# Graph layer with residual layernorm: W's product first, inside the stage that forms A, and A's unscaled blocks as the stationary operand

## Chip, cores, metric

One core of one Trainium2 chip. The metric is the device time of one execution in microseconds, and the median over the runs of a kernel. "PE" is TensorE's matmul side, "PEld" its weight loads, "DVE" VectorE, "ACT" ScalarE, "POOL" GpSimd, "SP" the engine that issues loads; "ACTq" and "SPq" are the queues on which transfers are issued. A run is fast when it lies within 1.5% of the fastest run of its kernel.

## The reference, cut to what matters

```python
B, N, F_IN, F_OUT = (8, 4096, 256, 256)                  # all float32
HW = jnp.einsum('bnf,fo->bno', H, W)                      # H is x
A_norm = jax.nn.relu((A + A.T) * 0.5)                     # A is adj, 4096 x 4096
D = jnp.sum(A_norm, axis=1)
d_inv_sqrt = jnp.where(D > 0, D_safe ** (-0.5), 0.0)
L_norm = jnp.eye(N) - d_inv_sqrt[:, None] * A_norm * d_inv_sqrt[None, :]
out = jnp.einsum('nm,bmo->bno', L_norm, HW)
return _layernorm(x + jax.nn.relu(out), axis=-1)
```

## The kernel before

It has two stages. The first forms A = relu((adj + adj.T)/2) in blocks of 512 x 512 (PE transposes, VectorE adds, ACT applies ReLU and sums the rows), writes A to DRAM and loads the first half of x. The second takes the batches in two halves and computes (x.T L), then W. P is 128, S is 512, A is 4, NS is 8, NB is 32, FC is 2, HB is 4.

```python
def symmetrise(i, j, tij, tji):                          # first stage, one block
    sym = spool.tile([P, A, S], F32, tag="sym", ...)      # 3 buffers
    for a in range(A):
        pt = psum.tile([P, S], F32, tag="ps", ...)
        for c in range(A):
            nc.tensor.transpose(pt[:, c*P:(c+1)*P], tji[:, c, a*P:(a+1)*P], ident)
        nc.vector.tensor_add(sym[:, a, :], pt, tij[:, a, :])
        m = i * A + a
        nc.scalar.activation(sym[:, a, :], sym[:, a, :], AF.Relu, scale=0.5,
                             accum_out=deg_parts[:, m, j:j+1])
    nc.scalar.dma_start(a_norm[i][j], sym)                # runs of 8 KB
# ... degrees, d^-1/2 as columns and along the free axis ...
for h in range(HALVES):                                   # second stage
    for j in range(NS):
        # pz: 8 PSUM banks, one for each (b, c)
        for i in range(NS):
            lt = npool.tile([P, A, S], F32, tag="lap", ...)
            nc.sync.dma_start(lt, a_norm[i][j])
            for a in range(A):
                m = i * A + a
                nc.vector.scalar_tensor_tensor(           # A scaled on the fly
                    lt[:, a, :], lt[:, a, :], ndinv[:, m:m+1], drow[:, j, :], ALU.mult, ALU.mult)
                # ... the identity is added on the diagonal ...
                for b in range(HB):
                    for c in range(FC):
                        nc.tensor.matmul(pz[b, c], lhsT=xt[h, m][:, b, c*P:(c+1)*P],
                                         rhs=lt[:, a, :], start=(m == 0), stop=(m == NB - 1))
        # ... pz is copied to zt; then, for each 128 rows, W's product:
        #     matmul(po, lhsT=zt[b, c][:, a*P:(a+1)*P], rhs=w_sb[:, c, :]),
        #     max(.,0) + x, layernorm, write
```

## Time and profile before

| | before |
|---|---|
| median | 4148.6 us (4 runs, 4146.7 to 4150.4) |
| first stage, to the first product with A | 397 us |
| products with A (8192 instructions) | 3516 us |
| W's products between them | 221 us |
| last layernorm and write | 13 us |
| bytes moved | 337 MB |

The four rows in the middle follow one another on the chain of work that ended last, so they add up to the span. The prediction shows the lines from which they come.

### The profile page before, as it was taken

The numbers are of one execution on the slowest core, as the hardware profiler recorded it, in microseconds if no ns is written. First come the engines' busy times: TensorE is split into PE (matmuls) and PEld (weight loads), VectorE is DVE, ScalarE is ACT, GpSimd is POOL, SyncE is SP. The second block draws the span as 40 slices with busy tenths as digits, with TensorE's granted clock in tenths as the row PEclk, the third lists the DMA queues.
The fourth block names the chain that finished last, engine by engine and source line by source line (L and its number), as shares of the span: only waits on it lengthen the run. The fifth ranks groups of instructions, "written<-read, shape, count | busy, mean of one in ns | idle before, by whom it ended". The sixth has DMA issues, their size and how long they took to land.

```text
span 4147.6 us, 24473 instructions
## 1 busy us (share of the span) xinstructions
PE 3912.8 (94%) x10272; PEld 1919.8 (46%) x10272; DVE 849.9 (20%) x1863; ACT 212.3 (5%) x585; POOL 75.7 (2%) x71
## 2 busy tenths in 40 slices
PE   4445999999999999999999999999999999999998
PEld 4344444454545444454545444454545444454544
DVE  3344112021212112021203112030302112020202
ACT  4444000000000000000000000000000000000000
POOL 0000000000000000000000000000000000000000
PEclk7667999999999999999999999999999999999999
DMA  9998111111111111111233101111111101111110
GB/s 391 407 389 310 41 41 51 41 51 41 51 41 51 41 40 52 41 51 41 76 117 107 41 36 56 41 51 41 51 41 50 41 32 60 38 54 41 51 41 21
DMA packets 129406, 337.40 MB, mean 81 GB/s; under 512 B 6160, under 2 KB 71952, under 8 KB 104720
## 3 DMA queue, kind: packets, MB, share of 16 engines
q1 hardware_dynamic: 86016, 234.90, 15.7%
q10 hardware_dynamic: 43280, 100.93, 6.4%
q8 instruction: 81, 1.33, 0.1%
q14 instruction: 29, 0.24, 0.0%
HBM read 235.14 MB, written 100.66 MB: 81 GB/s over the span
## 4 chain that ended last, share of the span: by engine, by line
PE 91%; DMA 7%; DVE 1%; SPq 1%; POOL 0%; issue 0%; ACT 0%; POOLq 0%; DVEq 0%; ACTq 0%
PE z L202 85%; PE o L154 5%; DMA adj<-in_adj_dram 5%; PE tr L85 1%; DMA a_norm<-sym 1%; DMA x<-in_x_dram 1%; DVE sym L88 1%; SPq L64 1%; SPq L74 0%; POOL dinv L128 0%; PE drow_ps L137 0%; ACT sym L90 0%; DVE y L170 0%; DVE y L161 0%; DVE stats L165 0%
## 5 line engine op out<-in xcount | busy, mean ns | idle before, releaser
L202 PE MATMUL z<-lap,x 128*128 128x512 f32 x8192 | 3518.3, 592 | 0.0
L202 PEld LDWEIGHTS z<-lap,x 128*128 128x128 f32 x8192 | 1556.4, 190 | 1952.4 <-issue 1935.6
L194 DVE SCALAR_TENSOR_TENSOR lap<-lap,ndinv,drow 128x512 f32<-128x512 f32 x512 | 354.4, 746 | 2651.4 <-DMA lap<-a_norm 2649.4
L85 PE MATMUL tr<-ident,adj 128*128 128x128 f32 x1024 | 170.7, 346 | 211.5 <-DMA adj<-in_adj_dram 211.5
L85 PEld LDWEIGHTS tr<-ident,adj 128*128 128x128 f32 x1024 | 163.8, 186 | 218.1 <-issue 210.3
L219 ACT COPY zt<-z 128x512 f32<-128x512 f32 x64 | 37.5, 586 | 3684.4 <-PE z L202 3684.4
L154 PE MATMUL o<-w_sb,zt 128*128 128x256 f32 x1024 | 223.6, 379 | 0.0
L154 PEld LDWEIGHTS o<-w_sb,zt 128*128 128x128 f32 x1024 | 194.6, 190 | 33.3 <-issue 7.7
L88 DVE TENSOR_TENSOR sym<-tr,adj 128x512 f32<-128x512 f32 x256 | 163.5, 686 | 219.8 <-PE tr L85 141.1
L90 ACT ACTIVATE sym<-sym 128x512 f32<-128x512 f32 x256 | 158.9, 622 | 213.4 <-DVE sym L88 168.3
L168 POOL TENSOR_TENSOR rstd<-rstd,neg_half 128x4 f32<-128x4 f32 x64 | 69.5, 1087 | 3680.8 <-DVE rstd L167 3676.4
L221 DVE COPY zt<-z 128x512 f32<-128x512 f32 x64 | 44.3, 692 | 337.0 <-PE z L202 337.0
L170 DVE TENSOR_SCALAR y<-y,mv,rstd 128x256 f32<-128x256 f32 x256 | 88.4, 409 | 59.7 <-POOL rstd L168 59.7
L165 DVE BATCH_NORM_STATS2 stats<-y 128x6 f32<-128x256 f32 x256 | 97.8, 410 | 1.1
L161 DVE SCALAR_TENSOR_TENSOR y<-o,x 128x512 f32<-128x512 f32 x128 | 86.0, 672 | 17.0 <-PE o L154 16.5
L90 ACT ACTIVATION_READ_ACCUMULATOR sym<-sym 128x1 f32 x256 | 47.9, 187 | 0.0
L166 DVE BATCH_NORM_AGGREGATE mv<-stats 128x2 f32<-128x6 f32 x256 | 42.9, 171 | 0.0
L199 DVE TENSOR_TENSOR lap<-lap,ident 128x128 f32<-128x128 f32 x64 | 15.8, 286 | 0.1
L137 PE MATMUL drow_ps<-ident,dinv 128*128 128x128 f32 x32 | 5.3, 341 | 10.0 <-DVE dinv L129 10.0
L128 POOL TENSOR_TENSOR dinv<-safe,neg_half 128x32 f32<-128x32 f32 x1 | 5.4, 5442 | 385.1 <-DMA a_norm<-sym 385.1
L167 DVE TENSOR_SCALAR rstd<-mv 128x4 f32<-128x4 f32 x64 | 10.5, 164 | 0.1
L137 PEld LDWEIGHTS drow_ps<-ident,dinv 128*128 128x128 f32 x32 | 5.1, 181 | 10.2 <-issue 10.2
(15 smaller groups left out, 7.9 us busy)
## 6 DMA issues: line engine op xcount, KB each, us to landing
lap<-a_norm SPq DMA_DIRECT2D x128, 1024.0 KB, 4.8
adj<-in_adj_dram SPq DMA_DIRECT2D x64, 1024.0 KB, 13.9
a_norm<-sym ACTq DMA_DIRECT2D x64, 1024.0 KB, 7.4
x<-in_x_dram SPq DMA_DIRECT2D x64, 512.0 KB, 9.2
out_dram<-y ACTq DMA_DIRECT2D x64, 512.0 KB, 2.9
w_sb<-in_L_gnn_W_dram ACTq DMA_DIRECT2D x1, 256.0 KB, 5.5
```

The source lines that it names most:

```text
L85: nc.tensor.transpose(pt[:, c * P : (c + 1) * P], tji[:, c, a * P : (a + 1) * P], ident)
L88: nc.vector.tensor_add(sym[:, a, :], pt, tij[:, a, :])
L90: nc.scalar.activation(sym[:, a, :], sym[:, a, :], AF.Relu, scale=0.5, accum_out=deg_parts[:, m, j : j + 1],)
L154: nc.tensor.matmul(po[:, b - b0, :], lhsT=zt[b, c][:, a * P : (a + 1) * P], rhs=w_sb[:, c, :], start=(c == 0), stop=(c == FC - 1),)
L161: nc.vector.scalar_tensor_tensor(y[:, b0 : b0 + 2, :], po, 0.0, xt[h, m][:, b0 : b0 + 2, :], ALU.max, ALU.add)
L165: nc.vector.bn_stats(stats[:, b, :], y[:, b, :])
L166: nc.vector.bn_aggr(mv[:, b, :], stats[:, b, :])
L168: nc.gpsimd.tensor_tensor(rstd, rstd, neg_half[:, :HB], ALU.pow)
L170: nc.vector.tensor_scalar(y[:, b, :], y[:, b, :], mv[:, b, 0:1], rstd[:, b : b + 1], ALU.subtract, ALU.mult,)
L194: nc.vector.scalar_tensor_tensor(lt[:, a, :], lt[:, a, :], ndinv[:, m : m + 1], drow[:, j, :], ALU.mult, ALU.mult)
L202: nc.tensor.matmul(pz[b, c], lhsT=xt[h, m][:, b, c * P : (c + 1) * P], rhs=lt[:, a, :], start=(m == 0), stop=(m == NB - 1),)
L221: nc.vector.tensor_copy(zt[b, c], pz[b, c])
```

## The change

W is applied first: G = x W costs the same arithmetic as applying it last. G needs x transposed (PE) and is scaled by r = d^-1/2 of its rows when it leaves PSUM; it is stored in DRAM. These "projections", one for each 128 rows of x, run inside the first stage, a round of the outer loop after the row sums that they need. In the second stage a 128 x 128 block of A, unscaled, is the stationary operand, and 512 columns of G are the moving one. The other scalings are applied to the results, so VectorE no longer scales L. G has 8 x 256 = 2048 columns, HG is half of them (1024), and e holds the row sums. Two smaller parts of the change: the row sums are a VectorE reduction instead of a by-product of ReLU (tested by act_sums), and adj has five buffers instead of four (not tested by itself). The intent was to take W's product and the scaling out of the stage where PE is the bound, and into one where PE was half idle.

The diff, cut to its core:

```diff
@@ first stage
-                nc.scalar.activation(sym[:, a, :], sym[:, a, :], AF.Relu, scale=0.5,
-                                     accum_out=deg_parts[:, m, j : j + 1])
-            nc.scalar.dma_start(a_norm[i][j], sym)
+            nc.scalar.activation(sym, sym, AF.Relu, scale=0.5)
+            nc.vector.tensor_reduce(part[:, i * A : (i + 1) * A, j * A : (j + 1) * A],
+                                    sym.rearrange("p a (c q) -> p a c q", q=P), AX.X, ALU.add)
+            nc.scalar.dma_start(a_dram[i][j].rearrange("(a p) s -> p a s", p=P), sym)   # runs of 2 KB
+        def project(m):
+            xin = xpool.tile([P, B, F], F32, tag="xin", ...)                            # 2 buffers
+            nc.sync.dma_start(xin, x[:, m * P : (m + 1) * P, :].rearrange("b p f -> p b f"))
+            xt = xpool.tile([P, B, FC, P], F32, tag="xt", ...)
+            for b in range(0, B, 2):
+                pt = psum.tile(...)
+                ...  nc.tensor.transpose(pt[:, k, c, :], xin[:, b + k, c * P : (c + 1) * P], ident)
+                nc.scalar.copy(xt[:, b : b + 2], pt)
+            g = xpool.tile([P, G], F32, tag="g", ...)
+            for b in range(0, B, 2):
+                ...  nc.tensor.matmul(pg[...], lhsT=xt[:, b + k, c, :], rhs=w_sb[:, c, :], ...)
+                nc.scalar.mul(g[:, b * FO : (b + 2) * FO], pg, r[:, m : m + 1])
+            nc.scalar.dma_start(g_dram[m], g)
+        todo = []
         for i in range(NS):
             for j in range(i, NS):
                 ...
+                for _ in range(-(-len(todo) // (NS - j))):
+                    project(todo.pop(0))
+            degrees(i)
+            todo += range(i * A, (i + 1) * A)
+        for m in todo:
+            project(m)
@@ second stage
+    for m in range(NB):
+        load_g(0, m)                                      # 33 buffers of 4 KB a partition
+    for h in range(HALVES):
+        for i in range(NB):
+            lt = lpool.tile([P, NB, P], F32, tag="l", ...)  # 2 buffers, loaded in runs of 512 bytes
+            for m in range(NB):
+                for c in range(HG // S):
+                    nc.tensor.matmul(py[c], lhsT=lt[:, m, :], rhs=gt[h, m][:, c * S : (c + 1) * S], ...)
+            # y = G e - py; relu(r y); + x; layernorm; write
-        # (the kernel before: scaling of L, x.T L, copies, W's product)
```

More of the change, by code (lines that the diff above doesn't have):

```diff
@@ L39 @@
     FC = F // P
+    G = B * FO
     HALVES = 2
     HB = B // HALVES
+    HG = G // HALVES
     EPS = 1e-5
     const = ctx.enter_context(tc.tile_pool(name="const", bufs=1))
-    xpool = ctx.enter_context(tc.tile_pool(name="xpool", bufs=NB + 1))
     dram = ctx.enter_context(tc.tile_pool(name="dram", bufs=1, space=bass.MemoryType.DRAM))
@@ L52 @@
     nc.scalar.dma_start(w_sb, w.rearrange("(c p) o -> p c o", p=P))
-    deg_parts = const.tile([P, NB, NS], F32, name="deg_parts")
+    part = const.tile([P, NB, NB], F32, name="part")
     neg_half = const.tile([P, NB], F32, name="neg_half")
     nc.vector.memset(neg_half, -0.5)
-    a_norm = [
-        [dram.tile([P, A, S], F32, name=f"a_norm_{i}_{j}") for j in range(NS)] for i in range(NS)
-    ]
-    xt = {}
-    def load_x(h, m):
-        xt[h, m] = xpool.tile([P, HB, F], F32, tag="x", name=f"x_{h}_{m}")
-        nc.sync.dma_start(
-            xt[h, m],
-            x[h * HB : (h + 1) * HB, m * P : (m + 1) * P, :].rearrange("b p f -> p b f"),
-        )
-    with tc.tile_pool(name="adj", bufs=4) as apool, tc.tile_pool(name="sym", bufs=3) as spool:
+    e = const.tile([P, NB], F32, name="e")
+    r = const.tile([P, NB], F32, name="r")
+    a_dram = [[dram.tile([S, S], F32, name=f"a_{i}_{j}") for j in range(NS)] for i in range(NS)]
+    g_dram = [dram.tile([P, G], F32, name=f"g_{m}") for m in range(NB)]
+    with (
+        tc.tile_pool(name="adj", bufs=5) as apool,
+        tc.tile_pool(name="sym", bufs=3) as spool,
+        tc.tile_pool(name="xin", bufs=2) as xpool,
+        tc.tile_pool(name="stat1", bufs=2) as stat1,
+    ):
         def load_adj(i, j):
@@ L88, in symmetrise @@
                 nc.vector.tensor_add(sym[:, a, :], pt, tij[:, a, :])
-                m = i * A + a
-                nc.scalar.activation(
-                    sym[:, a, :],
-                    sym[:, a, :],
-                    AF.Relu,
-                    scale=0.5,
-                    accum_out=deg_parts[:, m, j : j + 1],
-                )
-            nc.scalar.dma_start(a_norm[i][j], sym)
-        m = 0
+            nc.scalar.activation(sym, sym, AF.Relu, scale=0.5)
+            nc.vector.tensor_reduce(
+                part[:, i * A : (i + 1) * A, j * A : (j + 1) * A],
+                sym.rearrange("p a (c q) -> p a c q", q=P),
+                AX.X,
+                ALU.add,
+            )
@@ new lines, in symmetrise, with degrees @@
+            nc.scalar.dma_start(a_dram[i][j].rearrange("(a p) s -> p a s", p=P), sym)
+        def degrees(i):
+            ms = slice(i * A, (i + 1) * A)
+            deg = stat1.tile([P, A], F32, tag="deg", name=f"deg_{i}")
+            none = stat1.tile([P, A], F32, tag="none", name=f"none_{i}")
+            nc.vector.tensor_reduce(deg, part[:, ms, :], AX.X, ALU.add)
+            nc.vector.tensor_scalar(none, deg, 0.0, None, ALU.is_le)
+            nc.vector.tensor_add(e[:, ms], deg, none)
+            nc.gpsimd.tensor_tensor(r[:, ms], e[:, ms], neg_half[:, :A], ALU.pow)
@@ new lines, in project @@
+        def project(m):
+            xin = xpool.tile([P, B, F], F32, tag="xin", name=f"xin_{m}")
+            nc.sync.dma_start(xin, x[:, m * P : (m + 1) * P, :].rearrange("b p f -> p b f"))
+            xt = xpool.tile([P, B, FC, P], F32, tag="xt", name=f"xt_{m}")
+            for b in range(0, B, 2):
+                pt = psum.tile([P, 2, FC, P], F32, tag="ps", name=f"xtr_{m}_{b}")
+                for k in range(2):
+                    for c in range(FC):
+                        nc.tensor.transpose(pt[:, k, c, :], xin[:, b + k, c * P : (c + 1) * P], ident)
+                nc.scalar.copy(xt[:, b : b + 2], pt)
+            g = xpool.tile([P, G], F32, tag="g", name=f"gt_{m}")
+            for b in range(0, B, 2):
+                pg = psum.tile([P, 2 * FO], F32, tag="ps", name=f"pg_{m}_{b}")
+                for k in range(2):
+                    for c in range(FC):
+                        nc.tensor.matmul(
+                            pg[:, k * FO : (k + 1) * FO],
+                            lhsT=xt[:, b + k, c, :],
+                            rhs=w_sb[:, c, :],
+                            start=(c == 0),
+                            stop=(c == FC - 1),
+                        )
+                nc.scalar.mul(g[:, b * FO : (b + 2) * FO], pg, r[:, m : m + 1])
+            nc.scalar.dma_start(g_dram[m], g)
@@ L100 @@
+        todo = []
         for i in range(NS):
+            pairs = NS - i
             for j in range(i, NS):
@@ L106 @@
                     symmetrise(j, i, tji, tij)
-                if m < NB:
-                    load_x(0, m)
-                    m += 1
-        while m < NB:
-            load_x(0, m)
-            m += 1
-    p2 = ctx.enter_context(tc.tile_pool(name="p2", bufs=1))
-    npool = ctx.enter_context(tc.tile_pool(name="npool", bufs=3))
-    ypool = ctx.enter_context(tc.tile_pool(name="ypool", bufs=3))
-    stat = ctx.enter_context(tc.tile_pool(name="stat", bufs=4))
-    deg = p2.tile([P, NB], F32, name="deg")
@@ L121 @@
-    nc.vector.tensor_reduce(deg, deg_parts, AX.X, ALU.add)
-    pos = p2.tile([P, NB], F32, name="pos")
-    nc.vector.tensor_scalar(pos, deg, 0.0, None, ALU.is_gt)
-    safe = p2.tile([P, NB], F32, name="safe")
-    nc.vector.tensor_scalar(safe, pos, -1.0, 1.0, ALU.mult, ALU.add)
-    nc.vector.tensor_add(safe, safe, deg)
-    dinv = p2.tile([P, NB], F32, name="dinv")
-    nc.gpsimd.tensor_tensor(dinv, safe, neg_half, ALU.pow)
-    nc.vector.tensor_mul(dinv, dinv, pos)
-    ndinv = p2.tile([P, NB], F32, name="ndinv")
@@ L131 @@
-    nc.vector.tensor_scalar(ndinv, dinv, -1.0, None, ALU.mult)
-    drow = p2.tile([P, NS, S], F32, name="drow")
-    for j in range(NS):
-        pd = psum.tile([P, S], F32, tag="ps", name=f"drow_ps_{j}")
-        for a in range(A):
-            m = j * A + a
-            nc.tensor.transpose(
-                pd[:, a * P : (a + 1) * P], dinv[:, m : m + 1].to_broadcast([P, P]), ident
-            )
-        nc.scalar.copy(drow[:, j, :], pd)
-    def finish(h, j, zt):
-        for a in range(A):
-            m = j * A + a
-            y = ypool.tile([P, HB, FO], F32, tag="y", name=f"y_{h}_{m}")
-            stats = stat.tile([P, HB, 6], F32, tag="stats", name=f"stats_{h}_{m}")
-            mv = stat.tile([P, HB, 2], F32, tag="mv", name=f"mv_{h}_{m}")
-            rstd = stat.tile([P, HB], F32, tag="rstd", name=f"rstd_{h}_{m}")
-            for b0 in range(0, HB, 2):
-                po = psum.tile([P, 2, FO], F32, tag="ps", name=f"o_{h}_{m}_{b0}")
-                for b in (b0, b0 + 1):
-                    for c in range(FC):
-                        nc.tensor.matmul(
-                            po[:, b - b0, :],
-                            lhsT=zt[b, c][:, a * P : (a + 1) * P],
-                            rhs=w_sb[:, c, :],
-                            start=(c == 0),
-                            stop=(c == FC - 1),
-                        )
-                nc.vector.scalar_tensor_tensor(
-                    y[:, b0 : b0 + 2, :], po, 0.0, xt[h, m][:, b0 : b0 + 2, :], ALU.max, ALU.add
-                )
@@ new lines @@
+                for _ in range(-(-len(todo) // (NS - j))):
[4 more added lines that the diff above has]
+            project(m)
+    gpool = ctx.enter_context(tc.tile_pool(name="gpool", bufs=NB + 1))
+    lpool = ctx.enter_context(tc.tile_pool(name="lpool", bufs=2))
+    ypool = ctx.enter_context(tc.tile_pool(name="ypool", bufs=2))
+    stat = ctx.enter_context(tc.tile_pool(name="stat", bufs=4))
+    gt = {}
@@ new lines, in load_g @@
+    def load_g(h, m):
+        gt[h, m] = gpool.tile([P, HG], F32, tag="g", name=f"g_{h}_{m}")
+        nc.sync.dma_start(gt[h, m], g_dram[m][:, h * HG : (h + 1) * HG])
+    for m in range(NB):
+        load_g(0, m)
+    for h in range(HALVES):
+        for i in range(NB):
+            lt = lpool.tile([P, NB, P], F32, tag="l", name=f"l_{h}_{i}")
+            for s in range(NS):
+                nc.sync.dma_start(
+                    lt[:, s * A : (s + 1) * A, :],
+                    a_dram[s][i // A].rearrange("(a p) s -> p a s", p=P)[
+                        :, :, (i % A) * P : (i % A + 1) * P
+                    ],
+                )
+            xr = ypool.tile([P, HB, F], F32, tag="xr", name=f"xr_{h}_{i}")
+            nc.sync.dma_start(
+                xr, x[h * HB : (h + 1) * HB, i * P : (i + 1) * P, :].rearrange("b p f -> p b f")
+            )
+            py = [psum.tile([P, S], F32, tag="ps", name=f"py_{h}_{i}_{c}") for c in range(HG // S)]
+            for m in range(NB):
+                for c in range(HG // S):
+                    nc.tensor.matmul(
+                        py[c],
+                        lhsT=lt[:, m, :],
+                        rhs=gt[h, m][:, c * S : (c + 1) * S],
+                        start=(m == 0),
+                        stop=(m == NB - 1),
+                    )
+                if i == NB - 1 and h + 1 < HALVES and m < NB - 1:
+                    load_g(h + 1, m)
+            y = ypool.tile([P, HB, FO], F32, tag="y", name=f"y_{h}_{i}")
+            yf = y.rearrange("p b o -> p (b o)")
+            for c in range(HG // S):
+                nc.vector.scalar_tensor_tensor(
+                    yf[:, c * S : (c + 1) * S],
+                    gt[h, i][:, c * S : (c + 1) * S],
+                    e[:, i : i + 1],
+                    py[c],
+                    ALU.mult,
+                    ALU.subtract,
+                )
+            nc.scalar.activation(yf, yf, AF.Relu, scale=r[:, i : i + 1])
+            nc.vector.tensor_add(y, y, xr)
+            stats = stat.tile([P, HB, 6], F32, tag="stats", name=f"stats_{h}_{i}")
+            mv = stat.tile([P, HB, 2], F32, tag="mv", name=f"mv_{h}_{i}")
+            rstd = stat.tile([P, HB], F32, tag="rstd", name=f"rstd_{h}_{i}")
@@ L178, in finish @@
             nc.scalar.dma_start(
-                out[h * HB : (h + 1) * HB, m * P : (m + 1) * P, :].rearrange("b p f -> p b f"), y
+                out[h * HB : (h + 1) * HB, i * P : (i + 1) * P, :].rearrange("b p f -> p b f"), y
             )
-    for h in range(HALVES):
-        for j in range(NS):
-            pz = {
-                (b, c): psum.tile([P, S], F32, tag="ps", name=f"z_{h}_{j}_{b}_{c}")
-                for b in range(HB)
-                for c in range(FC)
-            }
-            for i in range(NS):
-                lt = npool.tile([P, A, S], F32, tag="lap", name=f"lap_{h}_{j}_{i}")
-                nc.sync.dma_start(lt, a_norm[i][j])
-                for a in range(A):
-                    m = i * A + a
-                    nc.vector.scalar_tensor_tensor(
-                        lt[:, a, :], lt[:, a, :], ndinv[:, m : m + 1], drow[:, j, :], ALU.mult, ALU.mult
-                    )
-                    if i == j:
-                        diag = lt[:, a, a * P : (a + 1) * P]
-                        nc.vector.tensor_add(diag, diag, ident)
-                    for b in range(HB):
-                        for c in range(FC):
-                            nc.tensor.matmul(
-                                pz[b, c],
-                                lhsT=xt[h, m][:, b, c * P : (c + 1) * P],
-                                rhs=lt[:, a, :],
-                                start=(m == 0),
-                                stop=(m == NB - 1),
-                            )
-                if h + 1 < HALVES and j == NS - 1 and i < NS - 1:
-                    for a in range(A):
-                        load_x(h + 1, i * A + a)
-                if h > 0 and j == 0 and i == 1:
-                    for a in range(A):
-                        load_x(h, (NS - 1) * A + a)
-            zt = {}
-            for k, (b, c) in enumerate(pz):
-                zt[b, c] = ypool.tile([P, S], F32, tag=f"zt_{b}_{c}", name=f"zt_{h}_{j}_{b}_{c}", bufs=1)
-                if k % 2 == 0:
-                    nc.scalar.copy(zt[b, c], pz[b, c])
-                else:
-                    nc.vector.tensor_copy(zt[b, c], pz[b, c])
-            finish(h, j, zt)
+        if h + 1 < HALVES:
+            load_g(h + 1, NB - 1)
 _INS = ["x", "adj", "L0_gnn_W"]
```

## The prediction

> **What bounds the kernel now.** I read the slices of the span first, then the chain that ended last in order of time, then the groups, then short stretches of the timeline. The slices show two stages with different limits (each column is a fortieth of the span, 104 us):
>
> ```profile
> PE   4445999999999999999999999999999999999998
> PEclk7667999999999999999999999999999999999999
> DMA  9998111111111111111233101111111101111110
> GB/s 391 407 389 310 41 41 51 41 51 41 51 41 51 41 40 52 41 51 41 76 117 107 41 36 56 41 51 41 51 41 50 41 32 60 38 54 41 51 41 21
> ```
>
> In the first stage (not quite four slices) the DMA engines are full at about 390 to 407 GB/s and PE is under half busy, at a granted clock of 0.6 to 0.7. After that PE is full at full clock and the DMA nearly idle. The chain in order of time (start us, us, what) gives the second stage exactly:
>
> ```profile
> 397.45 219.74 PE z L202 x512
> 617.18 13.81 PE o L154 x64
> ...
> 3900.64 219.73 PE z L202 x512
> ```
>
> Sixteen rounds of 219.74 + 13.81 us = 3736.8 us lead without a gap from 397.45 to 4134.2; the last 13.4 us to 4147.6 are the last layernorm and its write. So the first stage costs 397, W's product (L154) costs 16 x 13.81 = 221 on the path, and the adjacency product costs 3516. The groups (busy us, mean ns of one, idle before):
>
> ```profile
> L202 PE MATMUL z<-lap,x 128*128 128x512 f32 x8192 | 3518.3, 592 | 0.0
> L85 PE MATMUL tr<-ident,adj 128*128 128x128 f32 x1024 | 170.7, 346 | 211.5 <-DMA adj<-in_adj_dram 211.5
> L154 PE MATMUL o<-w_sb,zt 128*128 128x256 f32 x1024 | 223.6, 379 | 0.0
> L88 DVE TENSOR_TENSOR sym<-tr,adj 128x512 f32<-128x512 f32 x256 | 163.5, 686 | 219.8 <-PE tr L85 141.1
> L90 ACT ACTIVATE sym<-sym 128x512 f32<-128x512 f32 x256 | 158.9, 622 | 213.4 <-DVE sym L88 168.3
> ```
>
> The source has 4096 matrix products at L202 and the profile has 8192 instructions, so an f32 product is two instructions; at 219.74/512 = 429 ns each for 512 columns, and 13.81/64 = 216 ns for 256 columns. The mean duration (592) overlaps its neighbours and isn't the rate. VectorE's scaling of L (354 us busy) and the copies hide behind PE, so dropping them alone buys nothing.
>
> **What the Trainium skill says.** (1) "TensorE: Matmul & The Clock Gate", Part 1: the array starts at half clock and gets the full one after some 3.4 us of sustained work. Two stretches of one burst of transposes agree (stretch, length, busy time and count of each engine, clock, DMA, GB/s): 0.55, then 1.00, at 190 and then 107 ns per transpose.
>
> ```profile
> 375.20:378.70 3.50, 3.42 (x18) 3.45 (x19) 1.97 (x3) 1.44 (x4) 0.00 (x0) 0.55 0.54 219
> 378.70:382.30 3.60, 3.52 (x33) 3.28 (x31) 3.60 (x7) 3.47 (x12) 0.00 (x0) 1.00 0.82 346
> ```
>
> Part 4 of that page says that transposes don't bring the full clock; this trace shows that they do. (2) "DMA: Bandwidth & Descriptors", Issuing engines are not separate DMA queues: transfers issued by SP and ACT share the same engines. The trace agrees: reads of adj and x on one queue and writes of A on the other together make the 390 to 407 GB/s; so added bytes are added time in this stage. (3) "ScalarE: Activation LUTs", What ACT_TABLE_LOAD costs: an ACTIVATE with immediates takes 186 ns + 0.833 ns per element, a scale from memory adds about 93. 186 + 427 = 613 against 622 measured: it agrees.
>
> **The change part by part.** *Adjacency product.* Per half 32 row blocks x 32 column blocks x 2 groups of 512 columns: 4096 products of 128x128 by 512 again. Which operand is stationary swaps, the count, width and data type stay: 8192 x 0.429 = 3516 us, unchanged. Its loads are 64 x 2 MB, about 38 GB/s over 55 us per row block, in runs of 512 bytes instead of 8 KB; even at a third of the first stage's rate 2 MB take 16 us of 55. They stay hidden with two buffers.
>
> *W's product* leaves the second stage: -221 us. It reappears in the first as 32 projections (one per 128 rows of x), each of 16 new transposes of x and 16 products (32 instructions): 16 x 0.107 + 32 x 0.216 = 8.6 us of PE at full clock. A block of A costs 16 x 0.107 = 1.7 us.
>
> *Bytes of the first stage.* Before: adj 67.1 + A 67.1 + half of x 16.8 = 151 MB in 385 us = 392 GB/s. After: all of x (33.6) and its product written (33.6): 201.3 MB, at the same rate 513 us, +128. A block (1 MiB in, 1 MiB out) and a projection (the same) cost 5.35 us of DMA each.
>
> *The first stage by rounds of its outer loop*, the larger of DMA and PE in each, because the projections lag by a round. Round 0: 15 blocks, no projection: 80.3 us. Rounds 1 to 5: 13, 11, 9, 7, 5 blocks and 4 projections each: (13+4) x 5.35 = 91, then 80.3, 69.6, 58.9, 48.2, all DMA (PE of the last is 43). Round 6: 3 blocks, 4 projections: DMA 37.5, PE 39.5. Round 7: 1 and 4: DMA 26.8, PE 36.1. The last 4 projections stand alone: PE 34.4. Sum 428.3 + 110.0 = 538.3, and 7 for the first load to land (the first transpose starts at 7.1 now) is 545. I add 25 for waits between engines and stretches of PE below full clock, a guess of under 5%: **570 us**.
>
> *Other engines in that stage.* VectorE: four adds of 0.64 us start to start (163.5/256) and a new reduction of 2048 elements per block. From a reduction of 256 elements that took 0.42 us and about 1.04 ns per further element (0.746 us for 512 in the scaling, less a fixed part), I estimate 2.3 us: 4.8 x 64 = 310 us. ACT: 64 x (186 + 0.833 x 2048 = 1.9 us) + 128 copies x 0.59 + 128 scaled copies x 0.7 + 96 issues x 0.33 = 320. Both are below 513, but in round 0 VectorE (72 us) is close to the DMA (80).
>
> *Handover.* Now the first load of the second stage goes out when the last write of A has landed:
>
> ```profile
> 385.14 0.33 ACTq L97 DMA_DIRECT2D a_norm<-sym  x1
> ...
> 389.09 1.29 SPq L191 DMA_DIRECT2D lap<-a_norm  x3
> ```
>
> So 4 us for the write, 4.8 median for the load. The scaled product's tiles take over the first stage's memory in the same way: about **10 us** from the last projection to the first product, as what was 12 us before (385 to 397). The 31 further tiles follow at 1.3 us each while PE uses 1.7 us per tile, so they don't hold it.
>
> *Between the halves* the new tiles are loaded behind the products that free the old; the blocks of A may queue behind them: **4 us**, the latency of one load. *The end*: two evictions at 0.69, ReLU 1.1, add 1.2, four pairs of statistics 2.3, power 1.0, four normalisations 1.4, latencies, and 4 us for the write: **13 us** as before.
>
> Sum: 570 + 10 + 3516 + 4 + 13 = 4113; I say **4115 us**, 0.8% less. Of the 221 us taken out of the second stage some 185 come back in the first, mostly as bytes.
>
> **Rivals.** *A: the first stage runs engine after engine.* If each engine followed the source strictly, VectorE would wait for the whole block's ReLU before its reduction (2.6 + 2.1 + 2.3 = 7 us per block), and ACT would sit in that ReLU while PE waits for its copies of x; a pair of blocks and a projection would take about 21 us where the DMA needs 16. Over the 28 projections that is 140 more, some 710 for the stage and 4250 in all. Against it: the order is not the source's. Between the halves now the source has four loads of x after each load of L, yet further loads of L were issued ahead of them:
>
> ```profile
> 1991.02 27.79 SPq L191 DMA_DIRECT2D lap<-a_norm  x2
> 2039.17 20.97 SPq L64 DMA_DIRECT2D x<-in_x_dram  x4
> 2060.23 0.46 SPq L191 DMA_DIRECT2D lap<-a_norm  x1
> ```
>
> So work that is ready goes first, and 3 to 5 buffers per kind should keep the DMA full most of the time. *B: PE is the bound, cold.* With transposes at 0.167 us (170.7/1024 now) and W's products at 0.3, a projection takes 12.2 us, rounds 3 to 7 become PE-bound, and the stage takes about 620: 4165. For it: the clock of 0.6 to 0.7 now; against: PE will have shorter pauses. *C: ACT is held by issuing its writes.* A's write now has runs of 2 KB, like adj's load, whose issue took up to 7.7 us with full queues, while the 8 KB write always took 0.33. At 3 us for each of 64, ACT has 490 us, near the bound: 4130 to 4180. *D: the handover hides nothing.* If all 32 tiles of the product (16.8 MB, 43 us) come before the first block of A, it costs 50 instead of 10: 4155. *E: it overlaps better*, with a stage of 535 and no gap at the handover: 4070.
>
> **Range and chances.** E gives the low end, B and D together or a mild A the high end: 4070 to 4210. The 2% lines are 4067 and 4233. Faster needs a first stage below 525, hardly more than the bytes alone take: 0.05. Slower needs one of 690, the strict serial order: 0.10. Same: 0.85.
>
> **What would show it.** The adjacency product should be 8192 instructions at 429 ns, without idle time of PE beyond a few us per half; if its rate is another, the largest term is wrong. W's group should have moved into the first 14% of the span, at 216 to 300 ns each. The DMA row should be 9 for over five slices at about 390 GB/s; if it sits well lower there with PE below 9 too, rival A or C holds, and the waits of VectorE and ACT, or long issues on ACT's queue, tell which. If PE stands at 9 in the slices before the second stage with a clock of 0.7, it is B. A gap of over 20 us before the first adjacency product is D.

## The result

4108.4 us median (4 runs, 4104.2 to 4111.8) against 4148.6 before: ratio 0.9903, 95% interval 0.9889 to 0.9918. A ratio, here and below, is the mean time of one kernel's fast runs over that of the other's of the same rounds, so it is not quite the ratio of the medians. The profiled run spans 4105.6 us.

The slices of the changed kernel (a column is 103 us):

```profile
PE   5788999999999999999999999999999999999998
PEclk6899999999999999999999999999999999999999
DMA  9999872221111211211121621112222211111220
GB/s 382 398 403 405 318 283 62 62 62 53 41 61 61 62 62 62 62 44 49 62 61 62 220 62 59 39 57 62 62 62 62 62 48 45 62 62 62 62 62 11
```

The first stage now takes five and a half slices. The DMA is full for the first four. In the next two the mean falls to 318 and 283 GB/s while PE's row rises to 9. How the bound passes from bytes to PE is plainer in four stretches (stretch, length, busy time and count of PE, PEld, DVE, ACT, POOL, clock, DMA share, GB/s):

```profile
400.00:450.00 50.00, 46.16 (x286) 40.89 (x283) 24.81 (x30) 28.75 (x38) 1.01 (x1) 1.00 1.03 390
450.00:500.00 50.00, 45.55 (x251) 39.91 (x250) 17.56 (x22) 28.15 (x40) 1.41 (x2) 0.94 0.82 286
500.00:535.00 35.00, 35.00 (x192) 31.33 (x192) 0.00 (x0) 18.84 (x32) 0.60 (x1) 0.98 0.68 234
535.00:567.00 32.00, 31.45 (x170) 27.83 (x168) 0.00 (x0) 16.70 (x28) 0.00 (x0) 1.00 0.49 175
```

The DMA stays full to about 450 us, beside a PE that is over 90% busy. From 500 us on PE is busy nearly all the time, VectorE has nothing more to do, and the DMA moves 234 and then 175 GB/s, about half of the 400 from before. The chain in order of time shows where the path changes hands, and the handover to the second stage:

```profile
388.75 22.31 DMA xin<-in_x_dram
...
549.14 1.75 PE xtr L116 x16
550.89 6.91 PE pg L123 x32
557.79 1.75 PE xtr L116 x16
559.54 6.92 PE pg L123 x32
567.21 3.79 DMA g<-gt
571.64 4.27 DMA g<-g
576.15 3517.78 PE py L179 x8192
```

The transfer that ends at 411 us is the last one on the path of the first stage until its last write; from there on the path is PE with short pieces of VectorE and ACT. A projection is 16 transposes (1.75 us) and 32 product instructions (6.91 us); at the end they stand back to back, and the last eight come after the transposes of the last block of A. Then the last piece of G is written (3.79 us), the first is loaded (4.27 us), and all 8192 instructions of the product with A follow without a gap, between the halves of the batches as well. They end at 576.15 + 3517.78 = 4093.9; 11.7 us of layernorm and write remain.

The groups that answer to those shown of before (busy us, mean ns, idle before):

```profile
L179 PE MATMUL py<-g,l 128*128 128x512 f32 x8192 | 3517.8, 592 | 9.7 <-DMA g<-g 9.7
L123 PE MATMUL pg<-w_sb,xt 128*128 128x256 f32 x1024 | 251.1, 403 | 41.7 <-ACT xt L117 39.2
L86 PE MATMUL tr<-ident,adj 128*128 128x128 f32 x1024 | 140.4, 300 | 65.4 <-DVE sym L89 34.7
L91 DVE TENSOR_REDUCE part<-sym 128x16 f32<-128x2048 f32 x64 | 143.7, 2277 | 9.2 <-ACT sym L90 9.1
L90 ACT ACTIVATE sym<-sym 128x2048 f32<-128x2048 f32 x64 | 122.5, 1914 | 166.8 <-DVE sym L89 165.4
```

| | before | after | difference |
|---|---|---|---|
| up to the first product with A | 397.4 | 576.2 | +178.7 |
| products with A, and W's between them | 3736.8 | 3517.8 | -219.0 |
| end | 13.4 | 11.7 | -1.7 |
| span of the profiled run | 4147.6 | 4105.6 | -42.0 |

So of 219 us taken out of the second stage 179 came back in the first. The question for the experiments is what holds the first stage.

### The profile page after: what moved, and what is told of

It is laid out like the page before. It is cut to its first block, busy times and chain, and to the rows that moved or that the text cites. A ratio compares the mean times of both kernels' runs of the same rounds, so it can differ in the third digit from the quotient of the medians.

```text
span 4105.6 us, 25348 instructions
## 1 busy us (share of the span) xinstructions
PE 3965.0 (97%) x10752; PEld 1947.4 (47%) x10752; DVE 687.9 (17%) x1369; ACT 346.3 (8%) x385; POOL 73.2 (2%) x78
## 4 chain that ended last, share of the span: by engine, by line
PE 91%; DMA 6%; DVE 2%; ACT 1%; issue 0%; SPq 0%; ACTq 0%; POOLq 0%; DVEq 0%
PE py L179 86%; PE pg L123 4%; DMA a<-sym 2%; DMA adj<-in_adj_dram 2%; DVE sym L89 1%; DMA xin<-in_x_dram 1%; PE tr L86 1%; DMA l<-a 1%; PE xtr L116 1%; ACT sym L90 1%; DVE part L91 0%; ACT xt L117 0%; DMA g<-g 0%; DMA g<-gt 0%; DVE stats L205 0%
## 5 line engine op out<-in xcount | busy, mean ns | idle before, releaser
L179 PE MATMUL py<-g,l 128*128 128x512 f32 x8192 | 3517.8, 592 | 9.7 <-DMA g<-g 9.7
L179 PEld LDWEIGHTS py<-g,l 128*128 128x128 f32 x8192 | 1557.1, 190 | 1970.0 <-issue 1968.8
L191 DVE SCALAR_TENSOR_TENSOR y<-g,e,py 128x512 f32<-128x512 f32 x128 | 95.7, 748 | 3058.3 <-PE py L179 3051.3
L199 ACT ACTIVATE y<-y,r 128x1024 f32<-128x1024 f32 x64 | 73.5, 1148 | 3455.2 <-DVE y L191 3455.2
L123 PE MATMUL pg<-w_sb,xt 128*128 128x256 f32 x1024 | 251.1, 403 | 41.7 <-ACT xt L117 39.2
L123 PEld LDWEIGHTS pg<-w_sb,xt 128*128 128x128 f32 x1024 | 201.3, 201 | 85.3 <-ACT xt L117 57.1
L91 DVE TENSOR_REDUCE part<-sym 128x16 f32<-128x2048 f32 x64 | 143.7, 2277 | 9.2 <-ACT sym L90 9.1
L90 ACT ACTIVATE sym<-sym 128x2048 f32<-128x2048 f32 x64 | 122.5, 1914 | 166.8 <-DVE sym L89 165.4
L130 ACT ACTIVATE gt<-pg,r 128x512 f32<-128x512 f32 x128 | 87.7, 690 | 103.4 <-PE pg L123 99.9
L200 DVE TENSOR_TENSOR y<-y,xr 128x1024 f32<-128x1024 f32 x64 | 78.5, 1226 | 77.8 <-ACT y L199 77.8
```

Of the source, the lines that this page charges most:

```text
L90: nc.scalar.activation(sym, sym, AF.Relu, scale=0.5)
L91: nc.vector.tensor_reduce(part[:, i * A : (i + 1) * A, j * A : (j + 1) * A], sym.rearrange("p a (c q) -> p a c q", q=P), AX.X, ALU.add,)
L123: nc.tensor.matmul(pg[:, k * FO : (k + 1) * FO], lhsT=xt[:, b + k, c, :], rhs=w_sb[:, c, :], start=(c == 0), stop=(c == FC - 1),)
L130: nc.scalar.mul(g[:, b * FO : (b + 2) * FO], pg, r[:, m : m + 1])
L179: nc.tensor.matmul(py[c], lhsT=lt[:, m, :], rhs=gt[h, m][:, c * S : (c + 1) * S], start=(m == 0), stop=(m == NB - 1),)
L191: nc.vector.scalar_tensor_tensor(yf[:, c * S : (c + 1) * S], gt[h, i][:, c * S : (c + 1) * S], e[:, i : i + 1], py[c], ALU.mult, ALU.subtract,
```

## Experiments

Twelve kernels ran, each three times timed beside the kernel before on the same chip, and once more with a profile. **Theory T**: the bytes hold the first stage up to some 430 us, then PE's projections do. **R1**: the bytes and the waits around them hold all of it. **R2**: VectorE and ACT waiting for each other hold it.

### no_pe: the projection without PE

```diff
-            (transposes, copies, products, scaled copies)
+            nc.scalar.mul(g[:, b * FO : (b + 2) * FO], xin[:, b : b + 2, :], r[:, m : m + 1])
```

> Wrong result on purpose: the projection keeps its load of x, its ACT work and its write, but has no transpose and no product on PE (G = r*x). Theory T (the first stage is held by the bytes for some 430 us and by PE's projections in its last 130 us): with PE out of the way the stage is bytes alone, 206.5 MB (with the 5 MB of the second stage's loads that go out early) at 397 GB/s = 520, and the first adjacency product starts at about 537 instead of 576: total 4067 +- 10. Rival R1 (the bytes and the waits around them hold the whole stage, PE's end part is only where the last bytes happen to be): no more than 10 us gained, 4095 or more. Rival R2 (VectorE and ACT waiting for each other hold it): also 4095 or more.

Measured: 4070.1 us, ratio to before 0.9812 (0.9797 to 0.9826). The first product starts at 540.65 (chain of no_pe):

```profile
536.08 4.57 DMA g<-g
540.65 3518.52 PE py L166 x8192
```

T holds: without PE's part the stage is 35 us shorter and not shorter than its bytes (206.5 MB at 397 GB/s are 520 us, the estimate of the expectation). R1 and R2 as sole causes are out, since all transfers and all of VectorE's work were still there (ACT's work fell by 70 us, from 346 to 277, as the copies went with the transposes). What is left, 541 us, is the bytes and some 20 us of waits that no run takes apart. So of the 179 us that came back, 143 (541 less 397) are there without PE's projections, and 36 are PE's.

### act_sums: row sums on ACT, no VectorE reduction

```diff
-            nc.scalar.activation(sym, sym, AF.Relu, scale=0.5)
-            nc.vector.tensor_reduce(part[...], sym..., AX.X, ALU.add)
+                nc.scalar.activation(sym[:, a, :], sym[:, a, :], AF.Relu, scale=0.5,
+                                     accum_out=part[:, i * A + a, j : j + 1])
```

> Right result: ReLU per 128x512 slice with the row sums taken by ACT, as in the kernel before, instead of one ReLU over the whole block and a VectorE reduction (144 us of VectorE taken out, some 85 us of ACT added). Theory T: VectorE isn't on the path that sets the end, and the bytes stay: within 8 us of 4108. Rival R2 (the wait of VectorE for the block's ReLU and its reduction hold the first 400 us): 20 us or more faster, 4088 or less.

Measured: 4108.1 us, ratio 0.9904 (0.9889 to 0.9919). Taking 141 us of busy time off VectorE (687.9 to 546.6; ACT got 43 more) changed nothing. R2 is out, and in this kernel the new row sums cost nothing.

### no_xt, no_xt3 and x3: a smaller projection, and its control

```diff
# no_xt: the transposes and their copies are left out; the products read x as it is
-                            lhsT=xt[:, b + k, c, :],
+                            lhsT=xin[:, b + k, c * P : (c + 1) * P],
# no_xt3: as no_xt, and; x3: only this
-        tc.tile_pool(name="xin", bufs=2) as xpool,
+        tc.tile_pool(name="xin", bufs=3) as xpool,
```

> Wrong result on purpose: only the 16 transposes of x per projection and the 4 copies behind them are left out, the W products stay. A projection takes 6.9 us of PE instead of 8.65. Theory T: the nine projections that stand alone at the end and some of those just before are each 1.75 us shorter, 16 to 24 us in all: 4082 to 4092. R1 and R2: within 5 us of 4108.

Measured: 4097.0 us (4093.5 to 4103.0), ratio 0.9880: 11 us gained, less than T's 16. Its chain shows PE waiting for x in the part where it should have been the bound:

```profile
485.13 10.29 DMA xin<-in_x_dram
...
502.74 7.86 DMA xin<-in_x_dram
...
524.81 6.89 DMA xin<-in_x_dram
```

The edit did more than it should: the products now read x itself, so its two buffers come free later. Hence no_xt3, in whose trace nothing waits for x any more.

> Wrong result on purpose: no transposes of x, as in no_xt, but with three buffers for x instead of two. In no_xt the load of x has to wait for the W products that now read it directly, and PE waited 25 us for x between 485 and 532 us. Theory T with that as the cause of the small gain: those waits go, and the gain against 4108 is 16 to 24 us: 4084 to 4092. Rival (the bytes bound the end part more than T has it): 4094 or more, as without the third buffer.

Measured: 4079.0 us, ratio 0.9835 (0.9820 to 0.9850): 29 us under the changed kernel, above the 16 to 24 expected. In the changed kernel fifteen projections, not nine to thirteen, stand between 413 and 566 us, and 15 x 1.75 = 26. But no_xt3 differs from the changed kernel in the buffer too, so its control was needed.

> Right result: the changed kernel with three buffers instead of two for x, its transposes and the product, and nothing else. It is the missing control of no_xt3 (4079), which has the third buffer and no transposes. Theory T: at the end PE itself is the bound, 8.65 us for each projection, so that a further buffer gives nothing: within 6 us of 4108, and the 29 us of no_xt3 are the transposes of some 15 projections (1.75 us each). Rival (the third buffer, that is earlier loads of x, gave a good part of those 29): 4098 or less.

Measured: 4139.2 us (4137.7 to 4144.4), ratio 0.9980: 31 us slower than the changed kernel, which neither theory had. In the traces the order of instructions (waits for semaphores left out) is the same on PE, VectorE and ACT and differs on SP alone. The waits of x3 (who waited for whom: us in total, times, longest) and then its chain:

```profile
PE py L179 <- DMA l<-a: 49.5, 1, 49.5
```

```profile
549.47 6.92 PE pg L123 x32
557.13 3.79 DMA g<-gt
...
596.07 9.41 DMA l<-a
605.83 3518.35 PE py L179 x8192
```

PE's first stage ends 10 us earlier than in the changed kernel, but then PE waits 49.5 us. The first block of A for the second stage is loaded behind all 32 tiles of G (16.8 MB). In the changed kernel that block was loaded between 40 and 120 us. The first stage's buffers there take 40 + 24 + 48 = 112 KB of a partition and G's 33 tiles 132 KB, so that the blocks of A lie in memory that the first stage doesn't use; with 136 KB they share it and must wait for its end. This is my reading from the buffer sizes and SP's order; the 49.5 us are measured. The other traces agree with it: in the seven kernels with at most 112 KB (the changed one, act_sums, no_pe, no_xt, no_xt3, early, early_half) the first block of A was loaded at 37 to 54 us, and in x3 and the three resident kernels below, where its memory is shared too, only at the end of the first stage (596, 776, 609 and 506 us). It is the prediction's rival D, put at 50 us instead of 10. In no_xt3 there is no xt, the buffers are 112 KB again, and the load is early. What the third buffer is worth by itself therefore stays open: x3's last seven projections stand back to back at 8.65 us each, so it doesn't speed those, and its 10 us earlier end also has 4.2 MB less to load (the 16 pieces of A), which is 10 us at 400 GB/s.

### early: projections spread from the first round on

```diff
-                nc.scalar.mul(g[:, b * FO : (b + 2) * FO], pg, r[:, m : m + 1])
+                nc.scalar.copy(g[:, b * FO : (b + 2) * FO], pg)
-                for _ in range(-(-len(todo) // (NS - j))):
+                done += 2 if j > i else 1
+                while todo and (NB - len(todo)) * NS * NS < done * NB:   # todo = all 32 from the start
                     project(todo.pop(0))
     def load_g(h, m):
         ...
+        nc.scalar.mul(gt[h, m], gt[h, m], r[:, m : m + 1])
```

> Right result: W's product is stored unscaled, so that projections need no row sums and are spread evenly from the first round on; the scale r is applied by ACT to each tile of the product when it is loaded in the second stage. No byte and no PE work is added or taken away. Theory T: PE's work now lies beside the bytes, and no projections stand alone at the end: the first adjacency product at 535 to 545 instead of 576, total 4065 to 4080. R1 and R2: the bytes or the order hold the stage anyway, within 8 us of 4108.

Measured: 4075.1 us (4072.9 to 4075.5), right result, ratio 0.9822 (0.9807 to 0.9836). One stretch of early (columns as above) and then its chain:

```profile
400.00:500.00 100.00, 84.25 (x502) 73.30 (x502) 60.66 (x71) 51.76 (x67) 3.02 (x3) 0.97 1.05 402
```

```profile
538.42 4.19 DMA g<-g
544.07 3517.97 PE py L181 x8192
```

The same work in another order, with 64 scalings by ACT added in the second stage, saves 33 us. The DMA is now full up to 500 us; in the last 30 us of the stage it still falls to 276 and 211 GB/s. That is 5 us from no_pe, where PE had nothing to do in the projections. T holds. A part of the gain is given back at the handover, where PE waits 13.3 us (9.7 in the changed kernel), as the first tile of G has to be scaled as well.

### early_half: 16.8 MB less to write

```diff
-            nc.scalar.dma_start(g_dram[m], g)
+            nc.scalar.dma_start(g_dram[m], g[:, :HG])
```

> Wrong result on purpose: the spread projections (label early), but only the first half of each row of W's product is written, and both halves of the batches read it. Nothing else differs: 16.8 MB of writes are gone from the first stage. Theory T (with the projections spread, the first stage is as long as its bytes): 16.8 MB at 400 GB/s = 42 us off, 4033 +- 10. Rival (once spread, PE and the order of the engines are as close a bound as the bytes; PE was 0.74 to 0.88 busy there): 4055 or more.

Measured: 4036.8 us (4033.3 to 4042.1), ratio 0.9734 (0.9719 to 0.9748): 38 us less than early for 16.8 MB, where 42 were expected from the rate. The first product starts at 502.29. So once the projections are spread, bytes are time, at nine tenths of the rate.

### resident, resident2 and resident3: half of G never leaves the chip

The tiles of G for the first half of the batches are written where the second stage reads them, and scaled there when their row sums are known. That saves 16.8 MB of writes in the first stage (14.7 MB where 28 of the 32 tiles stay), with the right result. To make room, adj has four buffers, and x comes in pieces. The three versions differ from each other in several things at once, which the comments name; all three take row sums per 512 columns.

```diff
# resident: x in pieces of two batches (256 KB, 2 buffers); one buffer for g1
+            gt[0, m] = gpool.tile([P, HG], F32, tag="g", ...)      # opened before the first stage
+                g = gt[0, m] if b < HB else g1                     # g1, the second half, is written
# resident2: pieces of four batches (512 KB, 3 buffers); 28 of 32 tiles stay; transposes and
#            products of each pair of batches together; two buffers for g1
# resident3: as resident2, but all transposes of a piece before its products (so xt, which takes
#            their copies, holds four batches instead of two, still in 2 buffers)
```

> Right result: as the spread projections (label early), and the first half of W's product stays on chip, unwritten and unread in DRAM; x is loaded in pieces of two batches; row sums per 512 columns; the scale is applied in place. Theory T (where projections are spread, the first stage is as long as its bytes): 184.6 MB, no early loads of the second stage, at 397 GB/s = 465, + 7 for the first load, + some 10 of waits, + 9 for the handover: first adjacency product at 490 +- 12, total 4020 +- 15. Rival (spread projections end at what PE and the order of the engines allow, not at the bytes): no lower than 4060.

Measured: 4309.9 us, ratio 1.0391: far off. The slices of resident and then two of its waits:

```profile
GB/s 246 249 242 225 256 228 235 122 59 59 59 59 59 59 57 52 53 52 53 57 59 59 59 210 59 59 59 59 59 59 59 59 59 59 59 59 59 59 59 10
```

```profile
PE pg L127 <- ACT xt L123: 134.3, 128, 3.5
PE xtr L122 <- DMA xin<-in_x_dram: 113.4, 48, 6.2
```

The DMA was never full, at 225 to 256 GB/s. PE waited 48 times for a piece of x; I took this for the cause (two small buffers, too little of x in flight) and overlooked the longer wait, for ACT's copies of the transposes.

> Right result: as label resident, which came out at 4310 because its two buffers of 256 KB for x let the DMA fall to 240 GB/s while PE waited 113 us for x. Here x comes in pieces of 512 KB with three buffers, and four of the 32 product tiles go through DRAM to make room for them. Theory T with that as the cause: 186.7 MB at 397 GB/s = 470, + 7, + 10 of waits, + 9 for the handover: first product at about 496, total 4026 +- 20. Rival (something else in keeping the product on chip costs the time, such as the four buffers of adj instead of five or the scaling in place): 4150 or more.

Measured: 4144.3 us, ratio 0.9993, again far from theory's 4026. PE no longer waits for x, and 166 us are gained, but the other wait is still there (waits of resident2):

```profile
PE pg L136 <- ACT xt L132: 142.2, 128, 3.6
```

Each group of products waited for ACT's copy of the transposes made just before it: 128 waits of 1.1 us in the mean.

> Right result: as label resident2, which came out at 4144 with the DMA at 310 to 340 GB/s; there the transposes and the products of one pair of batches stood together, and PE waited 142 us in 128 waits for ACT's copy of the transposes just made. Here all transposes of a piece come before its products, as in the changed kernel. Theory T with that as the cause: the first stage is held by its 186.7 MB again, first product at about 496, total 4026 +- 20. Rival (the order of the engines with these smaller buffers holds the DMA down in another way): 4080 or more, that is no better than label early.

Measured: 4040.8 us (4038.2 to 4042.4), right result, ratio 0.9739 (0.9722 to 0.9755). The first four slices carry 384, 386, 383 and 379 GB/s, and the first product starts at 508.96 us (slices, then chain):

```profile
GB/s 384 386 383 379 342 84 63 63 63 40 55 63 62 63 63 46 48 63 63 63 63 50 211 63 63 63 63 55 39 63 63 63 63 60 35 63 63 63 62 11
```

```profile
508.96 3517.43 PE py L207 x8192
```

It is the fastest version with a right result, 2.6% under the kernel before and 1.6% under the changed one (4040.8 and 4108.4, of different rounds). PE's waits for ACT's copies fell from 142 to 66 us; whether the order or the larger xt did this, the runs don't separate. Before its first product PE stands 15.7 us, since the first block of A is loaded only after the last write of A has landed, as said under x3. The bytes are only a floor: two versions with the same plan, but smaller buffers or another order, were slower than the changed kernel.

### b_twicew and b_noscale: what the removed parts were worth

```diff
# b_twicew: the kernel before, every W product twice into the same sum
-                    for c in range(FC):
+                    for t in range(2 * FC):
+                        c = t % FC
# b_noscale: the kernel before, without VectorE's scaling of L and the added identity
-                    nc.vector.scalar_tensor_tensor(lt[:, a, :], lt[:, a, :], ndinv..., drow..., ...)
-                    if i == j: (identity)
```

> Wrong result on purpose: the kernel before with every W product computed twice into the same sum (1024 more instructions). Theory T: W's product lies fully on the path of the second stage, at 216 ns an instruction: +221 us, 4369 +- 6. Rival (part of it hides, so that moving it away was worth less than 221): 4340 or less.

Measured: 4365.8 us, 217 more than before; each round of W's product takes 27.63 us instead of 13.81, as here in the chain of b_twicew:

```profile
4080.43 27.63 PE o L155 x128
```

The chain's last round ends at 4327.78 + 27.64 = 4355.4, which is 4134.2 + 221; the end after it is 5 us shorter (4363.9 less 4355.4 is 8.5, before 13.4); why was not looked into. W's product lay fully on the path.

> Wrong result on purpose: the kernel before without VectorE's scaling of L and without the identity's addition (370 us of VectorE's busy time). Theory T: it lies beside PE, so only the first product starts some 3 us sooner: 4148, within 8. Rival (scaling of L held the loads of A or the products, and taking it off is part of the gain): 4130 or less.

Measured: 4150.3 us, ratio 1.0006 (0.9991 to 1.0021). VectorE's busy time fell by 356 us (849.9 to 494.0), and nothing was gained; not even the 3 us at the start, since the first product starts at 398.04. The scaling was hidden, and moving it is no part of the gain.

## Why the prediction was right

**Products with A unchanged**: right. 3516 predicted, 3517.8 measured, in the same 8192 instructions; swapping the stationary and the moving operand costs nothing. Loads of A in runs of 512 bytes stayed hidden: PE waited 9.7 us in all, at the start.

**W's product leaves 221 us**: right, shown by b_twicew.

**The first stage grows by about as much as it had**: right in the sum, and nearly so in its parts. Predicted were 570 us to the last projection, 10 for the handover: 580. Measured: 566.5 and 9.7, 576.2. The 12 us before, to which the prediction likened the handover, were another path: there the chain has 5.44 us of POOL's power and 5.27 us of PE's transposes of d^-1/2 after the write, not a load. The cost of a projection (8.6 us) and that of a block's transposes at full clock (1.7 us) were right to 0.05 us, and ReLU (1.9) and the reduction (2.3) to 0.03. "Mostly as bytes" was right too: 143 of the 179 us (no_pe).

**Where the bound changes**: the right mechanism, with its parts mis-sized. I had bytes up to round 5 (428 + 7 us) and PE for the 110 after it, with four projections alone at the end, and 25 us of waits. The instructions were ordered so that eight stood alone; the last wait for a transfer on the path ended at 411 us, and 155 us of mostly PE followed, although the DMA stayed full to about 450. The DMA row was 9 for four slices, not "over five". Nor had I seen that the second stage's first loads, 5.2 MB (16 pieces of A's blocks and two tiles of x), would go out in the first stage, at some 13 us of DMA. These errors and the guess of 25 us made up for each other (435 + 110 + 25 against 411 + 155); that 570 was so near is partly luck.

**Rivals.** A (engine after engine) is out by act_sums and no_pe. B (PE cold) didn't come: the clock was 0.67 in the first hundred microseconds, where the DMA was full (381 GB/s), 0.85 in the second and 0.91 to 1.00 from 200 us to the end of the stage. C (ACT held by its issues) is out: in the trace the 64 writes of A took 0.366 to 0.465 us to issue (before, 0.326 to 0.400, not "always" 0.33). D (everything of G before the first block of A) did not happen here, but one more buffer brought it about in x3. E was about early (4075), which it put at 4070.

**Between the halves** 4 us were predicted; there were none, since SP issued the blocks of A among the tiles of G. **The end**: 13 predicted, 11.7 measured.

## What to carry to other kernels

Before moving work out of a bound stage, price the stage that receives it in bytes and in each engine, round by round: here 219 us moved out and 179 came back. Work that depends on late results can pile up at the end, where nothing lies beside it; removing the dependence (here: store unscaled, scale at the load) gained 33 us, nearly as much as taking out all of PE's part of that work (38). Whether the next stage's first loads can go out early was here, as far as the traces tell, a matter of whose memory they reuse; one buffer more cost 31 us.

## What the Trainium skill lacked or had wrong

- "TensorE: Matmul & The Clock Gate", Part 4, says that transposes don't bring the full clock. In the kernel before, a burst of transposes alone went from a clock of 0.55 in its first 3.5 us to 1.00 in the next 3.6. The prediction's 190 and 107 ns each are busy time over count, in which a transpose at the edge counts twice; from start to start the trace has 213 and then 109 ns.
- The same page, Back-to-back issue gap, gives cycles by the number of columns and no time for float32 (how many passes float32 takes stands on another page, to which the section doesn't point). Here a float32 product is two instructions of 429 ns at 512 columns and of 216 ns at 256, at full clock: 858 ns against the page's 216 for 512 columns.
- No page says that the first loads of a stage can be held back by which buffers of the stage before their memory belonged to; x3 has one wait of 49.5 us, against 9.7 in the changed kernel, which is read so above.
